# A graph network's first relational layers: residual rows copied DRAM to DRAM, and layer 2's weight sums moved forward

## The chip, the cores and the metric

The kernel runs on one core of a Trainium2 chip. The time is the device time of one execution in microseconds; before the change it is 4654.29 us, the median of three runs (4651.23 to 4654.56). The profile is of one more execution. Its engines are TensorE (PE, with its weight loads as PEld), VectorE (DVE), ScalarE (ACT), GpSimd (POOL), and SyncE (SP), which issues most of the DMAs; POOL issues the indirect ones.

## The reference, cut to what matters

Four blocks are applied in a row to 10000 nodes of 512 features, all in float32: a relational graph network of two layers, a mixture of experts, a second graph network of four layers, and a quantised feed-forward. The change is in the first. With 5000 edges and 2 relations it computes

```python
def rgcn_gate_layer(x, row, col, edge_type, basis, att, gate_w, root, bias):
    w = jnp.einsum('rb,bio->rio', att, basis)      # 2 x 512 x 512 out of 30 bases
    x_j = x[col]
    for r in range(2):
        gate = sigmoid(x_j @ gate_w[r, :, 0])
        msgs.append(gate[:, None] * x_j @ w[r])
    msg = where(edge_type == 0, msgs[0], msgs[1])
    agg = segment_sum(msg, row, num_segments=10000)
    return agg + x @ root + bias

xn = layernorm(x)
h = relu(rgcn_gate_layer(xn, ..., basis1, att1, gate_w1, root1, bias1))
x = x + rgcn_gate_layer(h, ..., basis2, att2, gate_w2, root2, bias2)
```

## The kernel before, in words

**Node rows.** `rgcn_nodes1` goes over 20 blocks of up to 512 nodes. Each block is loaded from the input x (`rows_to`, L139), stored as it is to the DRAM tensor `a2_d` (that store is the "plain rows": the residual x, on which layer 2's results are added later), normalised (L170 to L181), stored to `xn_d`, transposed, multiplied with layer 1's root (L742), given the bias on POOL (L748), and stored to `r1_d`.

**Sorts.** Ahead of the nodes in the text, and interleaved with them in time, the edges are sorted twice by `sort_edges`, by source row and by target row: 40 steps each of small matmuls, ScalarE copies and short VectorE instructions (L334 to L356; L346 is one of these).

**Relation weights.** `relation_weights` (L625 to L638) makes the two 512 x 512 matrices of a layer. For each of 30 bases it loads 1 MB on SP's queue (L630) into one of two buffers and adds it, scaled, to each matrix: one VectorE instruction of 128 x 2048 per matrix (L635 for the first basis, L637 for the others). So there are 60 loads and 120 sums for the two layers.

**Edges.** `rgcn_edges` runs once per layer over 41 tiles of 128 sorted edges. Its loop, whose order on PE, POOL, ACT and DVE is kept as written, has four steps that run on different tiles at a time: `fetch` gathers the source rows by an indirect DMA on POOL (L614; from `xn_d` in layer 1, from `r1_d` in layer 2), six tiles ahead; `make_ready` forms the gates on VectorE and ScalarE (L669 to L682); `add_up` sums rows of the same target by a matmul (L689) and copies the sums on ScalarE (L693); `put` multiplies by the relation's matrix (L703), copies the product (L708) and adds it into DRAM by an indirect DMA on POOL (`scatter_add`, L619; into `r1_d` in layer 1, into `a2_d` in layer 2). After each iteration one step of a side job may be taken, `next(beside)`: steps of `place_nodes`, a generator of short PE and VectorE instructions that lays out rows for the later graph network (L405 to L567).

**Order.** Everything not in such a loop is ordered by a scheduler ahead of the run: each engine has one fixed queue, in which what comes earlier in the program text goes first when it can, and what comes later fills the gaps. Even in the edge loop, instructions from later text can be put between those of the loop. In the text the order is: sorts, nodes, layer 1's weights, layer 1's edges, layer 2's weights, layer 2's edges. SP's queue is one fixed order as well: a load that waits for its buffer holds up what stands behind it.

Of the kernel before, what the change touches and what calls it, by code (L numbers as in the profile page):

```python
# [17 lines left out]
P = 128  # L18
# [24 lines left out]
CAP = 625  # L43
CT = (CAP + P - 1) // P
LAYERS = 4
FETCHED, READY = 6, 3
LN_EPS = 1e-5
BN_EPS = 1e-5
# [21 lines left out]
def gnn_ffn_kernel(ctx: ExitStack, tc: tile.TileContext, I, out, dram):  # L70
# [70 lines left out]
    def row_broadcast(pool, d, width, name):  # L141

        t = pool.tile([P, width], F32, name=name)
        nc.sync.dma_start(t, bass.AP(tensor=d.tensor, offset=d.offset, ap=[[0, P], [1, width]]))
        return t
# [467 lines left out]
    def gather(dst, src, idx):  # L613
        return nc.gpsimd.indirect_dma_start(  # L614
            out=dst, out_offset=None, in_=src, in_offset=bass.IndirectOffsetOnAxis(ap=idx, axis=0)
        )
# [6 lines left out]


    def relation_weights(basis, att_d, pool, stream, tag):  # L625
        att = row_broadcast(pool, att_d, RELATIONS * BASES, f"att_{tag}")
        ws = pool.tile([P, RELATIONS, KC * D], F32, name=f"w_{tag}")
        for b in range(BASES):
            t = stream.tile([P, KC, D], F32, name="basis")
            nc.sync.dma_start(t, basis[b].rearrange("(k p) o -> p k o", p=P))  # L630
            tf = t.rearrange("p k o -> p (k o)")
            for r in range(RELATIONS):
                c = att[:, r * BASES + b : r * BASES + b + 1]
                if b == 0:
                    nc.vector.tensor_scalar(ws[:, r], tf, c, None, op0=OP.mult)  # L635
                else:
                    nc.vector.scalar_tensor_tensor(ws[:, r], tf, c, ws[:, r], op0=OP.mult, op1=OP.add)  # L637
        return ws  # L638

    def rgcn_edges(tag, meta, src_d, relu, ws, gate_d, dst_d, beside, take):  # L640

        with ExitStack() as s:
# [12 lines left out]

            def fetch(t):
                got[t] = wk.tile([P, D], F32, name="x", bufs=FETCHED + 2)
                gather(got[t], src_d, meta["gidx"][:, t : t + 1])  # L660

            def make_ready(t):
                x, kt = got[t], meta["key"][:, t : t + 1]
# [48 lines left out]
            with tc.manual_schedule(engines={E_.PE, E_.Pool, E_.Activation, E_.DVE}):  # L712
                for i in range(RT + FETCHED):
                    if i < RT:
                        fetch(i)
                    if i >= FETCHED - 1 and i - FETCHED + 1 < RT:
                        add_up(i - FETCHED + 1)
                    if i >= FETCHED:
                        put(i - FETCHED)
                    if READY <= i < RT + READY:  # L720
                        make_ready(i - READY)
                    if take(i):
                        next(beside, None)

    def rgcn_nodes1(root, bias, pools):


        ld, tp, small, pt, po = pools
        for b in range(NB):
            tiles, parts, cols = block_tiles(b), block_parts(b), block_cols(b)  # L730
            x = ld.tile([P, 4, D], F32, name="x_in")
            rows_to(x, I["x"], b)
            rows_to(x, a2_d, b, store=True)
            xn = ld.tile([P, 4, D], F32, name="xn")
            layernorm(small, xn, x, tiles, parts, on_act=True)
            rows_to(xn, xn_d, b, store=True)
            xT = transposed(tp, pt, xn, tiles, cols, on_act=True)
            o = tp.tile([P, 4, D], F32, name="o_nodes")
            for a, n in tiles:
                ps_o = po.tile([P, D], F32, name="ps_o")  # L740
                for k in range(KC):
                    nc.tensor.matmul(  # L742
                        ps_o[:n], lhsT=xT[:, k, a * P : a * P + n], rhs=root[:, k, :],
                        start=k == 0, stop=k == KC - 1,
                    )
                nc.scalar.copy(o[:n, a, :], ps_o[:n])
            for n, a0, a1 in parts:
                nc.gpsimd.tensor_tensor(  # L748
                    o[:n, a0:a1], o[:n, a0:a1], bias[:n, None, :].to_broadcast([n, a1 - a0, D]), OP.add
                )  # L750
            rows_to(o, r1_d, b, store=True)

    with ExitStack() as s:
        wpool = s.enter_context(tc.tile_pool(name="w_rel", bufs=1))
        stream = s.enter_context(tc.tile_pool(name="stream", bufs=2))
        src_meta = s.enter_context(tc.tile_pool(name="src_meta", bufs=1))
        wk = s.enter_context(tc.tile_pool(name="sort", bufs=1))
        place_wk = s.enter_context(tc.tile_pool(name="place_wk", bufs=1))
        ps = s.enter_context(tc.tile_pool(name="sort_ps", bufs=2, space=PSUM))
        with ExitStack() as n:  # L760
            ld = n.enter_context(tc.tile_pool(name="ld1", bufs=2))
            tp = n.enter_context(tc.tile_pool(name="tp1", bufs=2))
            fix = n.enter_context(tc.tile_pool(name="fix1", bufs=1))
            small = n.enter_context(tc.tile_pool(name="small1", bufs=3))
            pt = n.enter_context(tc.tile_pool(name="pt1", bufs=2, space=PSUM))
            po = n.enter_context(tc.tile_pool(name="po1", bufs=3, space=PSUM))
            zero = fix.tile([P, D], F32, name="zero")
            nc.gpsimd.memset(zero, 0.0)
            for d in (r1_d, a2_d, xf_d, x2_d):
                clear_spare(zero, d)  # L770
            root = load_square(fix, I["L0_gnn_root1"], "root")
            bias = row_broadcast(fix, I["L0_gnn_bias1"], D, "bias")
            by_src = sort_edges(
                "s", I["src"], I["dst"], I["edge_type_2"], by_src_d, wk, ps, src_meta, by_relation=True
            )
            by_src = add_targets(by_src, wk, ps, src_meta)
            by_dst = sort_edges(
                "d", I["dst"], I["src"], I["edge_weight1"].rearrange("e o -> (e o)"), by_dst_d, wk, ps,
                meta_pool,
            )  # L780
            rgcn_nodes1(root, bias, (ld, tp, small, pt, po))
            ws = relation_weights(I["L0_gnn_basis1"], I["L0_gnn_att1"], wpool, stream, "1")
        placing = place_nodes(by_dst, place_wk, ps, meta_pool)
        rgcn_edges(
            "1", by_src, xn_d, False, ws, I["L0_gnn_gate_w1"], r1_d, placing,
            lambda i: i >= FETCHED and i % 2 == 0,
        )
        ws = relation_weights(I["L0_gnn_basis2"], I["L0_gnn_att2"], wpool, stream, "2")
        rgcn_edges("2", by_src, r1_d, True, ws, I["L0_gnn_gate_w2"], a2_d, placing, lambda i: True)
        for _ in placing:  # L790
            pass

# [1048 lines left out]
```

## Time and profile before

| what | value |
|---|---|
| runs | 4654.29 us median, 4651.23 to 4654.56, three runs |
| profiled execution | 4630.97 us; its span 4629.2 us, mean granted TensorE clock 0.932 |
| busy in the span | PE 4040.4 us (87%), DVE 2791.9 (60%), ACT 1722.2 (37%), POOL 1566.0 (34%) |
| first matmul of the edges, layer 1 | 549.70 us |
| layer 1's edges, first gather to last scatter-add | 532.76 to 840.90 us |
| layer 2's edges, first gather to last scatter-add | 846.62 to 1096.89 us |
| one basis sum (L637) | 2.34 us median, 2.31 to 6.90, 116 of them from 33.2 to 625.0 us |
| SP's queue from 0 to 700 us | 148.03 MB, 62.7% of 16 DMA engines |

The profile shows one execution. A span is the time from its first to its last instruction. "Idle before" an instruction is the time in which its engine did nothing, and the name behind it is what is taken to have ended that; when the engine named had long been done, the wait was for something else, often a DMA. A time "to landing" is from a DMA's issue until its data is there. PE's busy time is modelled, so it can look fuller than it is.

### The profile page before, as it was taken

What the parts mean: (1) busy time and instruction counts of PE and PEld (TensorE: products, weight loads), DVE (VectorE), ACT (ScalarE), POOL (GpSimd) and SP (SyncE); (2) the same over time, 40 slices, a digit from 0 to 9 for tenths busy, and PEclk for the clock granted to TensorE, in tenths of its full rate; (3) what the DMA queues carried; (4) which work ended last, traced back from release to release, by engine and by line L of the source; (5) the groups of instructions that cost most, each with busy time, mean ns of one, the idle gap of its engine ahead of it and who ended that gap; (6) DMA issues with size and microseconds to landing.
All of it is one profiled execution on the core that took longest, in us unless ns stands there. A gap on an engine that the chain in (4) does not pass through costs nothing.

```text
span 4629.2 us, 42910 instructions
## 1 busy us (share of the span) xinstructions
PE 4040.4 (87%) x13624; PEld 2049.1 (44%) x13624; DVE 2791.9 (60%) x5866; ACT 1722.2 (37%) x3082; POOL 1566.0 (34%) x1128
## 2 busy tenths in 40 slices
PE   6799568897999954987788999999999999999997
PEld 4443234443444422443444555545554455544443
DVE  7888864554545456746655557545575455755776
ACT  4334112232333312115545423353233632334775
POOL 3434334342000035875552114211142111422443
PEclk9899789898989876998899999999999999999998
DMA  8677654456555423987521223102231013301332
GB/s 281 227 262 254 215 129 89 82 105 165 197 175 179 153 71 82 163 154 228 176 66 43 78 91 102 37 25 78 97 96 33 30 76 107 88 28 48 109 111 97
DMA packets 294560, 558.83 MB, mean 121 GB/s; under 512 B 41376, under 2 KB 72129, under 8 KB 293311
## 3 DMA queue, kind: packets, MB, share of 16 engines
q1 hardware_dynamic: 221072, 367.30, 23.5%
q0 software_dynamic: 73264, 188.79, 17.7%
q8 instruction: 111, 1.82, 0.2%
q14 instruction: 113, 0.93, 0.1%
HBM read 295.03 MB, written 260.95 MB: 120 GB/s over the span
## 4 chain that ended last, share of the span: by engine, by line
PE 39%; DVE 8%; DMA 3%; ACT 2%; issue 2%; POOL 2%; POOLq 0%; DVEq 0%; ACTq 0%
PE ps_b L1337 15%; PE ps_d L1337 9%; PE ps_o L1613 5%; PE ps_e L1337 4%; PE ps_x L1444 2%; PE ps_x L1268 2%; DMA x<-xg_d,gpos 2%; DVE stats L1422 1%; DMA x_in<-x_d,node_at 1%; PE ps_q L1681 1%; ACT feat L1433 1%; DVE feat L1272 1%; DVE x L1257 1%; DVE feat L1352 1%; DVE t L1360 0%
## 5 line engine op out<-in xcount | busy, mean ns | idle before, releaser
L1337 PE MATMUL ps_b<-feat,w 128*128 128x512 f32 (+1 forms) x1120 | 497.5, 585 | 25.5 <-ACT feat L1433 25.5
L1337 PE MATMUL ps_d<-feat,w_s 128*128 128x512 f32 (+1 forms) x1120 | 503.1, 586 | 2.0 <-ACT p L1345 1.5
L1345 ACT ACTIVATE feat<-ps_b,cols 128x512 f32<-128x512 f32 (+1 forms) x300 | 203.5, 682 | 552.3 <-PE ps_b L1337 539.6
L1372 POOL TENSOR_TENSOR feat<-feat 128x1024 f32<-128x1024 f32 (+1 forms) x70 | 162.6, 2322 | 622.0 <-DVE feat L1371 621.6
L1385 POOL TENSOR_TENSOR feat<-feat,p 128x1024 f32<-128x1024 f32 (+1 forms) x70 | 177.4, 2534 | 482.9 <-ACT feat L1345 482.7
L637 DVE SCALAR_TENSOR_TENSOR w<-basis,att,w 128x2048 f32<-128x2048 f32 x116 | 315.7, 2730 | 15.3 <-DMA basis<-in_L_gnn_basis 15.3
L742 PE MATMUL ps_o<-root,xT 128*128 128x512 f32 (+1 forms) x632 | 322.9, 623 | 0.0
L1337 PEld LDWEIGHTS ps_b<-feat,w 128*128 128x128 f32 x1120 | 208.6, 191 | 256.4 <-issue 209.7
L703 PE MATMUL ps_o<-w,aT 128*128 x656 | 306.8, 612 | 0.1
L1446 DVE TENSOR_TENSOR x_rows<-ps_x,be 128x512 f32<-128x512 f32 (+1 forms) x237 | 157.4, 685 | 230.9 <-PE ps_x L1444 230.9
L1337 PEld LDWEIGHTS ps_d<-feat,w_s 128*128 128x128 f32 x1120 | 203.1, 192 | 199.6 <-issue 176.8
L918 PE MATMUL ps_n<-root,rT 128*128 128x512 f32 (+1 forms) x632 | 287.8, 611 | 0.0
L1337 PE MATMUL ps_b<-t,w_s 128*128 128x512 f32 (+1 forms) x560 | 258.3, 602 | 28.0 <-ACT feat L1345 28.0
L1337 PE MATMUL ps_e<-feat,w 128*128 128x512 f32 (+1 forms) x560 | 259.0, 602 | 9.3 <-DVE feat L1303 9.3
L614 POOL DMA_INDIRECT x<-xg_d,gpos x160 | 179.1, 1120 | 251.4 <-issue 55.2
L1337 PE MATMUL ps_b<-feat,w_s 128*128 128x512 f32 (+1 forms) x560 | 250.2, 586 | 0.0
L1433 ACT ACTIVATE feat<-feat,bn_sm 128x512 f32<-128x512 f32 (+2 forms) x320 | 236.4, 806 | 3.4 <-DVE bn_sm L1552 3.4
L1422 DVE BATCH_NORM_STATS2 stats<-feat 128x6 f32<-128x512 f32 (+1 forms) x320 | 203.0, 667 | 47.6 <-POOL feat L1385 34.6
L1268 PEld LDWEIGHTS ps_x<-same,x 128*128 128x128 f32 x1280 | 165.7, 197 | 106.3 <-ACT x L1263 47.7
L1268 PE MATMUL ps_x<-same,x 128*128 128x128 f32 x1280 | 172.5, 284 | 43.2 <-ACT x L1263 32.0
L1371 DVE TENSOR_TENSOR feat<-feat,t 128x1024 f32<-128x1024 f32 (+1 forms) x70 | 83.8, 1198 | 197.5 <-PE ps_b L1337 197.5
L170 DVE BATCH_NORM_STATS2 ln_st<-x_in 128x6 f32<-128x512 f32 (+1 forms) x237 | 159.5, 682 | 59.3 <-DMA x_in<-x_d,node_at 55.6
(487 smaller groups left out, 7663.9 us busy)
## 6 DMA issues: line engine op xcount, KB each, us to landing
basis<-in_L_gnn_basis SPq DMA_DIRECT2D x60, 1024.0 KB
xg_d<-x_rows SPq DMA_DIRECT2D x234, 256.0 KB
xg_d<-x_in SPq DMA_DIRECT2D x39, 512.0 KB
x_in<-in_x SPq DMA_DIRECT2D x19, 1024.0 KB
a_d<-x_in SPq DMA_DIRECT2D x19, 1024.0 KB
xn_d<-xn SPq DMA_DIRECT2D x19, 1024.0 KB
r_d<-o_nodes SPq DMA_DIRECT2D x19, 1024.0 KB
r_in<-r_d SPq DMA_DIRECT2D x19, 1024.0 KB
```

The lines of the kernel that those rows point to most:

```text
L614: return nc.gpsimd.indirect_dma_start(out=dst, out_offset=None, in_=src, in_offset=bass.IndirectOffsetOnAxis(ap=idx, axis=0))
L637: nc.vector.scalar_tensor_tensor(ws[:, r], tf, c, ws[:, r], op0=OP.mult, op1=OP.add)
L703: nc.tensor.matmul(ps_o, lhsT=aT[:, k, :], rhs=w_all[:, bass.ds(w0 + k * D, D)], start=k == 0, stop=k == KC - 1,)
L742: nc.tensor.matmul(ps_o[:n], lhsT=xT[:, k, a * P : a * P + n], rhs=root[:, k, :], start=k == 0, stop=k == KC - 1,)
L918: nc.tensor.matmul(ps_o[:n_], lhsT=rT[:, k, a * P : a * P + n_], rhs=root[:, k, :], start=k == 0, stop=k == KC - 1,)
L1268: nc.tensor.matmul(ps_a[:, k, :], lhsT=x[:, k * P : (k + 1) * P], rhs=same, start=True, stop=True)
L1337: nc.tensor.matmul(ps[fo], lhsT=A[a][:, k, fo * P : (fo + 1) * P], rhs=x[:, k, :], start=first and k == 0, stop=k == 1, skip_group_check=True,
L1345: nc.scalar.activation(dst[:, fo, :], ps[fo], func, bias=b, scale=scale)
L1385: nc.gpsimd.tensor_tensor(b22, b22, p5, OP.add)
L1422: nc.vector.bn_stats(stats[:, k, 2 * p + j, :], big[:, k, s0 + j * w : s0 + (j + 1) * w])
L1433: nc.scalar.activation(hb, hb, AF.Relu, bias=sm[:, fo, 3:4], scale=sm[:, fo, 2:3])
L1613: nc.tensor.matmul(ps_o[:n_], lhsT=big[:, kc, t * P : t * P + n_], rhs=W2[kc], start=kc == 0, stop=kc == KC - 1,)
```

## The change

There are four edits. (1) The store of plain rows to `a2_d` leaves the node blocks. In its place the first 40 iterations of layer 1's edge loop each issue one DMA on SP's queue from DRAM to DRAM, 250 rows of x into `a2_d`; each waits for the gather that its iteration fetched. (2) `relation_weights` becomes a generator that does one basis per step. Layer 1's 30 and the first 24 of layer 2's are now written ahead of the edge loop, inside the first part. (3) The other six of layer 2's are written into layer 1's edge loop, one in each of the iterations 8, 14, 20, 26, 32 and 38; steps of `place_nodes` are taken in the odd iterations from 7 on, where before it was the even ones from 6 on. Layer 2's edge loop takes a step in every iteration, as before. (4) There are three buffers for bases in place of two.

```diff
+EARLY_BASES = 24
     def relation_weights(basis, att_d, pool, stream, tag):
         att = row_broadcast(pool, att_d, RELATIONS * BASES, f"att_{tag}")
         ws = pool.tile([P, RELATIONS, KC * D], F32, name=f"w_{tag}")
-        for b in range(BASES):
-            t = stream.tile([P, KC, D], F32, name="basis")
-            nc.sync.dma_start(t, basis[b].rearrange("(k p) o -> p k o", p=P))
...
-        return ws
+        def sums():
+            for b in range(BASES):
+                t = stream.tile([P, KC, D], F32, name="basis")
+                nc.sync.dma_start(t, basis[b].rearrange("(k p) o -> p k o", p=P))
...
+                yield
+        return ws, sums()
...
             def fetch(t):
                 got[t] = wk.tile([P, D], F32, name="x", bufs=FETCHED + 2)
-                gather(got[t], src_d, meta["gidx"][:, t : t + 1])
+                return gather(got[t], src_d, meta["gidx"][:, t : t + 1])
...
                 for i in range(RT + FETCHED):
                     if i < RT:
-                        fetch(i)
+                        fetched = fetch(i)
...
-                    if take(i):
-                        next(beside, None)
+                    beside(i, fetched)
...
             rows_to(x, I["x"], b)
-            rows_to(x, a2_d, b, store=True)
...
-        stream = s.enter_context(tc.tile_pool(name="stream", bufs=2))
+        stream = s.enter_context(tc.tile_pool(name="stream", bufs=3))
...
-            ws = relation_weights(I["L0_gnn_basis1"], I["L0_gnn_att1"], wpool, stream, "1")
+            ws1, adding = relation_weights(I["L0_gnn_basis1"], I["L0_gnn_att1"], wpool, stream, "1")
+            for _ in adding:
+                pass
+            ws2, adding = relation_weights(I["L0_gnn_basis2"], I["L0_gnn_att2"], wpool, stream, "2")
+            for _ in range(EARLY_BASES):
+                next(adding)
         placing = place_nodes(by_dst, place_wk, ps, meta_pool)
+        def beside_1(i, ready):
+            if i > FETCHED and i % 6 == 2:
+                next(adding, None)
+            elif i > FETCHED and i % 2:
+                next(placing, None)
+            if i < ET:
+                c0, c1 = N * i // ET, N * (i + 1) // ET
+                cp = nc.sync.dma_start(a2_d[c0:c1, :], I["x"][c0:c1, :])
+                tc.add_manual_dep(
+                    cp.ins, ready.ins.name,
+                    mybir.DependencyInfo(mybir.DependencyClass.Sync, mybir.DependencyReason.DATA),
+                    reason="not all at once, and not beside the nodes",
+                )
+        rgcn_edges("1", by_src, xn_d, False, ws1, I["L0_gnn_gate_w1"], r1_d, beside_1)
+        for _ in adding:
+            pass
         rgcn_edges(
-            "1", by_src, xn_d, False, ws, I["L0_gnn_gate_w1"], r1_d, placing,
-            lambda i: i >= FETCHED and i % 2 == 0,
+            "2", by_src, r1_d, True, ws2, I["L0_gnn_gate_w2"], a2_d, lambda i, _: next(placing, None)
         )
-        ws = relation_weights(I["L0_gnn_basis2"], I["L0_gnn_att2"], wpool, stream, "2")
-        rgcn_edges("2", by_src, r1_d, True, ws, I["L0_gnn_gate_w2"], a2_d, placing, lambda i: True)
```

More of the change, by code (lines that the diff above doesn't have):

```diff
@@ L627, in relation_weights, with rgcn_edges @@
         ws = pool.tile([P, RELATIONS, KC * D], F32, name=f"w_{tag}")
-        for b in range(BASES):
-            t = stream.tile([P, KC, D], F32, name="basis")
[L630 to L637, printed above, removed]
-        return ws
-    def rgcn_edges(tag, meta, src_d, relu, ws, gate_d, dst_d, beside, take):
+        def sums():
+            for b in range(BASES):
+                t = stream.tile([P, KC, D], F32, name="basis")
+                nc.sync.dma_start(t, basis[b].rearrange("(k p) o -> p k o", p=P))
+                tf = t.rearrange("p k o -> p (k o)")
+                for r in range(RELATIONS):
+                    c = att[:, r * BASES + b : r * BASES + b + 1]
+                    if b == 0:
+                        nc.vector.tensor_scalar(ws[:, r], tf, c, None, op0=OP.mult)
+                    else:
+                        nc.vector.scalar_tensor_tensor(ws[:, r], tf, c, ws[:, r], op0=OP.mult, op1=OP.add)
+                yield
+        return ws, sums()
+    def rgcn_edges(tag, meta, src_d, relu, ws, gate_d, dst_d, beside):
         with ExitStack() as s:
```

## The prediction

> **What bounds the kernel now.** I read the windows by stage first, since a share over 4.6 ms says little about a change that ends before 1.1 ms. The columns are busy time (and instructions) of PE, PEld, DVE, ACT and POOL, then granted clock, DMA share and GB/s.
>
> ```profile
> 0.00:408.00 408.00, 339.78 (x1180) 163.87 (x1181) 336.73 (x752) 160.22 (x345) 155.47 (x92) 0.94 0.76 256
> 446.00:532.00 86.00, 63.26 (x189) 29.49 (x187) 66.58 (x41) 22.57 (x41) 33.26 (x9) 0.89 0.69 218
> 532.00:628.00 96.00, 35.35 (x105) 20.01 (x105) 85.83 (x102) 8.49 (x19) 29.19 (x17) 0.64 0.67 201
> 628.00:846.00 218.00, 182.68 (x675) 99.45 (x675) 101.81 (x392) 45.16 (x105) 90.52 (x67) 0.94 0.48 84
> ```
>
> Up to about 510 us TensorE works nearly without a break on the node rows and the two sorts: this is the first part. From 532 to 628 layer 1's edges have begun, but TensorE is busy 35 of 96 us and VectorE 86 of 96; the clock falls to 0.64. After 628 VectorE is half idle. The same windows for the basis sums alone (L637; VectorE busy, instructions) say why:
>
> ```profile
> 408.00:446.00 38.00, 14.02 (x7) 1.00 0.80 273
> 446.00:532.00 86.00, 62.62 (x21) 0.89 0.69 218
> 532.00:628.00 96.00, 73.22 (x32) 0.64 0.67 201
> ```
>
> 32 of layer 2's 60 sums fall into the opening of layer 1's edges, between the edge instructions of the same engine. SyncE's queue shows it too: 15 of the 60 basis loads are issued from 528 to 616 us.
>
> ```profile
> 522.15 1.14 SPq L139 DMA_DIRECT2D r_d<-o_nodes  x2
> 528.18 87.95 SPq L630 DMA_DIRECT2D basis<-in_L_gnn_basis  x15
> ```
>
> Then the timeline of POOL, for what sets the pace of the edges once VectorE is free (start, duration, instruction, idle time before it):
>
> ```profile
> 532.76 3.00 POOL L614 DMA_INDIRECT x<-xn_d,gidx_s  x1 [17.95 <-DVE w L637]
> ...
> 818.84 1.58 POOL L619 DMA_INDIRECT r_d<-o,sidx  x1 [4.00 <-DMA r_d<-o,sidx]
> 824.34 1.55 POOL L619 DMA_INDIRECT r_d<-o,sidx  x1 [3.92 <-issue]
> 829.89 1.55 POOL L619 DMA_INDIRECT r_d<-o,sidx  x1 [4.00 <-ACT o L708]
> 835.35 1.55 POOL L619 DMA_INDIRECT r_d<-o,sidx  x1 [3.92 <-issue]
> 840.90 1.55 POOL L619 DMA_INDIRECT r_d<-o,sidx  x1 [4.00 <-DMA r_d<-o,sidx]
> 846.62 1.01 POOL L614 DMA_INDIRECT x<-r_d,gidx_s  x1 [4.18 <-DMA r_d<-o,sidx]
> ```
>
> The last six scatter-adds have no gathers between them and still start 5.5 us apart: 1.55 of issue and 4.0 of waiting. The engines named differ from row to row and the wait doesn't, so it is the landing of the scatter before, which adds into the same DRAM tensor. The free stage runs at this pace with gathers too, one tile per 5.5 to 5.7 us. So layer 1's edges are bound twice: by VectorE to 628 us, then by a chain of scatter-adds.
>
> **The change part by part.** All sums are made against the profiled execution (4630.97 us; span 4629.2 and 1.8 around it). The median of the runs is 4654.29, 23.3 above it, and I carry a difference over unchanged. A change under 0.2% (9.3 us) can't be told from none here.
>
> *Bases out of the opening of the edges.* Before, 34 sums (17 bases) were left when the edges opened: 86 us (541 to 627) in which 8 tiles were made ready (eight pairs of L669), 5.06 us a base. At the free pace 8 tiles cost 8 x 5.55 = 44 us, so the bases cost 42 us. The two layers agree: from first to last scatter-add layer 1 takes 840.90 - 566.37 = 274.5 us and layer 2, with as many tiles, 1096.89 - 867.00 = 229.9, 44.6 less. If n early bases are still unsummed when the edges open, n x 5.06 us pass in which 0.47 n tiles are made ready, so the saving is 42 - 2.45 n. Six bases go to single tiles. So n is 17 - 6 = 11 if the first part takes no more than before (15 us saved), and 0 if all of the 24 fit (42 saved; 58 from first gather to last scatter-add by layer 2's length, 250.3 against 308.1, since the ramp to the first scatter-add also shrinks from 33.6 to 20.4 us). Does the first part have room? Up to 510 us VectorE is busy about 410, so about 100 are idle, and 11 bases need 22 x 2.34 = 51. Half of the idle time lies in gaps of 1 to 2 us behind TensorE's sort products, shorter than a sum; the start and the waits for the sorted lists can't be filled. I take n = 5: **-29 us**, ends -15 and -58.
>
> *Third basis buffer.* L637 waits 15.3 us for loads in all, 11 times; with one more load in flight the waits before the edges (6.8 us) shrink. It also frees SyncE: the last two r_d stores stood behind a basis load at 521.73 that waited for its buffer, though POOL had finished the rows at 514.8. Gathers could start some us earlier: **-3 us**, ends 0 and -8.
>
> *More sums in the first part.* TensorE there waits 22.1 us for L346, a short sort instruction that on VectorE can stand behind a 2.34 us sum. Twelve more sums among the sorts at up to 1.2 us each would be 15; most of the added ones come after the sorts end at 446. I take **+3**, ends 0 and +15.
>
> *Plain rows out of the first part.* 21 stores of up to 1 MB (20.5 MB) leave SyncE's queue and the engines. In that part TensorE waits for no input row (0.7 us of VectorE waits for x_in in all), so I book nothing; the relief is part of the room for n.
>
> *Forty copies beside layer 1's edges.* Each moves 250 rows, 512 KB, from x to a2_d, and waits in SyncE's queue for gather i to land. Behind the waiting copy stand the loads of the last six bases and layer 2's gate; a wait lasts at most one tile, and three of the six loads find free buffers early, so I cost it at nothing; were each of the six sums to wait one tile, 33 us. Layer 2's scatter-adds need all copies, but the last gather is issued at 804 and the first of these scatter-adds at 867, so 60 us cover it. What is dear is the scatter chain, which stands at 5.5 us with the DMA engines half busy. Gathers land 4.3 us after issue, and one is issued 1.9 us after each scatter-add, so a copy is issued 6.2 us after one scatter-add, that is 0.7 us after the next: it runs while that one is in flight. No row shows a DRAM-to-DRAM copy. Two rows bound it:
>
> ```profile
> 820.38 0.34 SPq L144 DMA_DIRECT2D gate<-in_L_gnn_gate_w  x1
> ```
> ```profile
> 1030.46 0.37 SPq L149 DMA_DIRECT2D root<-in_L_gnn_root  x1
> ```
> ```profile
> 1031.63 1.58 POOL L619 DMA_INDIRECT a_d<-o,sidx  x1 [2.90 <-ACT o L708]
> 1033.52 0.99 POOL L614 DMA_INDIRECT x<-r_d,gidx_s  x1 [0.30 <-issue]
> 1041.21 1.59 POOL L619 DMA_INDIRECT a_d<-o,sidx  x1 [6.70 <-ACT o L708]
> ```
>
> The gate load, 512 KB like a copy, was issued 1.5 us after the scatter-add of 818.84, and the next came 5.5 us after it: no delay. Root, bias and the small loads behind them (some 1.6 MB) began 1.2 us before a scatter-add, which landed after 8.8 us instead of 4.8: 4.0 more, 2.5 us per MB, so 1.3 us for half a MB. Here a rule speaks against the change. The Trainium skill ("DMA: Bandwidth & Descriptors", section "Why a DMA increments its semaphore by 16 and not by 1") says that a transfer uses as many engines, up to 16, as divide its slowest dimension. 250 rows would give 10. The first 700 us moved 148.03 MB on SyncE's queue for 62.7% of 16 engines, 21 GB/s an engine; ten engines then need 2.4 us a copy, not 1.5, and as a scatter-add is complete only with its slowest engine, it could wait up to 2.4 us. The same page ("Queues, rings and completion order") has an engine drain a packet of some 9 to 17 descriptors of one queue before it turns to the other: 16 rows of 2 KB are 1.5 us. By these rules 34 copies (seven are released by the first gathers, before any scatter-add) cost 34 x 1.5 = 51 us or more, up to 82; by the gate row nothing. The trace can't decide, as no load there has 250 rows. I take a value near the gate row, for it has the copy's size and nearly its phase, and because the chain gives way: a copy that delays a gather comes later behind the next scatter-add. 0.2 us each: **+7 us**, ends 0 and +82.
>
> *Late bases.* Six times two sums, 4.7 us, on VectorE in tiles without a placing step. VectorE waits 2.4 to 3.3 us per tile there for ScalarE's gate; the rest, up to 2.3, reaches an activation with one tile of slack. **+4**, ends 0 and +14.
>
> Sum: -29 - 3 + 3 + 7 + 4 = **-18 us**: 4613 for a profiled execution, 4636 for the median.
>
> **The rivals.** (1) *The copies lengthen the scatter chain.* For it: the 8.8 us landing, the two rules, the engines half busy already. Against: the gate row, and the opening of the edges itself, where basis loads ran at 200 GB/s and two scatter-adds landed after 5.0 and 5.4. At 1.5 us a copy: -18 - 7 + 51 = +26, 4680; it decides from 25 / 34 = 0.74 us a copy, and at 2.4 gives +57. (2) *The early bases don't fit.* n stays 11 and the sums slow the sorts: -15 - 3 + 15 + 7 + 4 = +8 at worst, -4 with the sorts unharmed; about 4655. For it: VectorE is at 83% there already and its order is fixed before the run. The change then doesn't do what it says, for the edges open as crowded as before. (3) *All 24 fit and the ramp shrinks*: -58 + 3 + 7 + 4 - 3 = -47, 4607. For it: 100 us of idle VectorE and 20 MB less to move. (4) *A late basis load stands behind copies* and VectorE stops the edges: up to +33 on my sum, +15, 4669.
>
> **How the numbers follow.** My sum 0.42, rival 1 0.24, rival 2 0.17, rival 3 0.12, rival 4 0.05. Faster by over 0.2%: 0.38 of mine, 0.12 of (3), 0.04 of (2): 0.54. Within 0.2%: 0.04 of mine, 0.08 of (2), 0.02 of (1): 0.14. Slower: 0.32. The predicted time is my sum's, 4636; its own range is 4620 to 4646. The range reaches to rival 3 below, 4600, and above to rival 1 at about 1.8 us a copy, 4690.
>
> **What would show it.** The windows from the first gather: TensorE busy well over 35 of its first 96 us, and a clock above 0.64. L637: few sums between the first gather and the first ten scatter-adds, then pairs six tiles apart. First to last scatter-add of layer 1: 245 to 255 us instead of 274.5. The scatter-adds 5.5 to 5.9 us apart beside the copies; 7 or more shows rival 1. The first gather between 522 and 540; later, with more TensorE waits for L346, shows rival 2. VectorE waiting for a basis load inside the edges shows rival 4. I am wrong if layer 1's edges end later than 846 us.

## The result, and the profile after

The changed kernel takes 4638.22 us (median of 20 runs, 4629.52 to 4653.54) against 4651.83 us of the kernel before on the same chip (20 runs, 4641.55 to 4670.19). The ratio is 0.9974 with a 95% interval of 0.9965 to 0.9983, or 8 to 16 us less. The forecast was 4636 us. It is right as a total, and that by luck: three of its terms are wrong, and they cancel.

Single executions scatter by some 10 us, and the two profiled ones don't show the gain (4637.62 us after, 4630.97 before; the last section has what is known of the reason). So I compare stages by their marks, in us from the start of the span. The line numbers of the changed kernel: basis load L634, basis sum L641, gather L615, scatter-add L620, copy L801.

| mark | before | after | difference |
|---|---|---|---|
| last bias addition of the node rows ends | 514.8 | 517.1 | +2.3 |
| first gather of layer 1 | 532.76 | 531.84 | -0.9 |
| first scatter-add of layer 1 | 566.37 | 549.08 | -17.3 |
| last scatter-add of layer 1 | 840.90 | 824.58 | -16.3 |
| median spacing of these scatter-adds | 5.70 | 6.66 | +0.96 |
| last scatter-add of layer 2 | 1096.89 | 1074.96 | -21.9 |

The marks are of one execution each, and by the end of layer 2 they show more than the 8 to 16 us that the timed runs gain.

First the windows by stage of the changed kernel, with the columns as before (busy time and instructions of PE, PEld, DVE, ACT and POOL; granted clock, DMA share, GB/s):

```profile
0.00:408.00 408.00, 339.90 (x1187) 166.64 (x1188) 369.49 (x755) 160.24 (x340) 145.98 (x88) 0.96 0.72 244
446.00:532.00 86.00, 66.23 (x191) 27.63 (x190) 65.66 (x68) 20.22 (x42) 37.29 (x16) 0.90 0.68 220
532.00:628.00 96.00, 75.28 (x269) 43.74 (x270) 48.90 (x169) 19.85 (x45) 40.74 (x31) 0.88 0.69 182
628.00:846.00 218.00, 149.75 (x536) 83.78 (x535) 106.50 (x336) 38.08 (x87) 86.78 (x59) 0.84 0.59 141
```

The opening of the edges has changed as foreseen: TensorE is busy 75 of 96 us where it was 35, at a clock of 0.88 where it was 0.64. The room was found in the first 408 us: VectorE is busy 369 us there (337 before), and TensorE no less than before. The stage after 628 has become slower: TensorE does 536 matmuls in 218 us where it did 675, since fewer of layer 1's 41 scatter-adds are left for it (28, where it had 36) and they come further apart. The DMA engines are busy 0.59 of it, up from 0.48.

The basis sums alone, in the same kernel (VectorE busy, instructions):

```profile
0.00:408.00 408.00, 197.07 (x76) 0.96 0.72 244
408.00:446.00 38.00, 21.65 (x8) 0.96 0.58 202
446.00:532.00 86.00, 59.87 (x22) 0.90 0.68 220
532.00:628.00 96.00, 9.21 (x4) 0.88 0.69 182
```

In the kernel before, 58 sums lay in the first 408 us (165.84 us of VectorE); now 76 do. The 24 early bases are all summed when the first gather goes; the four sums from 532 to 628 are the first two of the six late bases. So all 24 fit, as rival 3 had it.

SyncE's queue and the scatter-adds on POOL, where one late basis is loaded:

```profile
535.34 141.22 SPq L801 DMA_DIRECT2D a_d<-in_x  x26
676.66 0.53 SPq L634 DMA_DIRECT2D basis<-in_L_gnn_basis  x1
685.27 35.22 SPq L801 DMA_DIRECT2D a_d<-in_x  x6
720.58 0.54 SPq L634 DMA_DIRECT2D basis<-in_L_gnn_basis  x1
```
```profile
662.85 1.59 POOL L620 DMA_INDIRECT r_d<-o,sidx  x1 [3.79 <-DMA r_d<-o,sidx]
...
669.41 1.59 POOL L620 DMA_INDIRECT r_d<-o,sidx  x1 [3.68 <-DVE eq L213]
...
675.97 1.59 POOL L620 DMA_INDIRECT r_d<-o,sidx  x1 [3.52 <-ACT aT L699]
...
685.42 3.24 POOL L620 DMA_INDIRECT r_d<-o,sidx  x1 [6.57 <-DMA r_d<-o,sidx]
```

Scatter-adds beside copies start 6.56 us apart here, and the one after the basis load of 676.66 starts 9.45 us after its predecessor. That next one takes 3.24 us to issue in place of 1.59, while VectorE does the two sums (684.84 to 689.46 us); so it is with each scatter-add whose issue starts during a sum in this kernel (2.86 to 3.24 us). In the waits of the stage, the scatter-add's for its predecessor and VectorE's for a late basis both have a row (total, times, longest):

```profile
POOL r_d L620 <- DMA r_d<-o,sidx: 60.3, 15, 6.6
...
DVE w L641 <- DMA basis<-in_L_gnn_basis: 19.6, 3, 9.3
```

So rival 1 (copies lengthen the chain) is there at 0.96 us a copy, and rival 4 (VectorE waits for a late load) three times, 9.3, 5.4 and 4.9 us.

To put a price on each, I take what every gap between layer 1's scatter-adds has over the undisturbed 5.7 us and add these up. Before: 46.5 us, of which 43.1 in the first twelve gaps (sums in the opening, single gaps of 22 and 24 us). After: 47.5 us, spread over the stage. Sums out of the opening therefore gave 17.3 + 43.1 = 60 us, and what was new beside the edges cost 47.5 - 3.4 = 44. The difference is the 16 us by which layer 1 ends earlier.

Not all of these 44 us belong to copies and late bases. Two gaps near the end are 9.21 us (beside the last copy and small loads, `sw` and `sb`, that the kernel before issued in layer 2's edges) and 8.43 us (beside no transfer; a `place_nodes` instruction of 3.45 us on VectorE covers the start of POOL's issue, which takes 4.46 us). The two hold 6.2 us over the pace.

### The profile page after: what moved, and what is told of

It reads as the page before. It is cut to its first block, busy times and chain, and to the rows that moved or that the text cites. A ratio compares the mean times of both kernels' runs of the same rounds, so it can differ in the third digit from the quotient of the medians.

```text
span 4635.8 us, 42956 instructions
## 1 busy us (share of the span) xinstructions
PE 4036.5 (87%) x13624; PEld 2049.5 (44%) x13624; DVE 2788.0 (60%) x5866; ACT 1724.1 (37%) x3082; POOL 1560.6 (34%) x1128
## 3 DMA queue, kind: packets, MB, share of 16 engines
q1 hardware_dynamic: 212016, 367.30, 23.5%
## 4 chain that ended last, share of the span: by engine, by line
PE 38%; DVE 8%; DMA 3%; issue 2%; ACT 2%; POOL 2%; POOLq 0%; DVEq 0%; ACTq 0%
PE ps_b L1361 15%; PE ps_d L1361 9%; PE ps_o L1637 5%; PE ps_e L1361 4%; PE ps_x L1468 2%; PE ps_x L1292 2%; DMA x<-xg_d,gpos 2%; DVE stats L1446 1%; DMA x_in<-x_d,node_at 1%; PE ps_q L1705 1%; DVE feat L1296 1%; ACT feat L1457 1%; DVE feat L1376 1%; DVE x L1281 1%; DVE t L1384 1%
## 5 line engine op out<-in xcount | busy, mean ns | idle before, releaser
L1361 PE MATMUL ps_b<-feat,w 128*128 128x512 f32 (+1 forms) x1120 | 497.5, 585 | 25.6 <-ACT feat L1457 25.6
L641 DVE SCALAR_TENSOR_TENSOR w<-basis,att,w 128x2048 f32<-128x2048 f32 x116 | 306.2, 2651 | 19.6 <-DMA basis<-in_L_gnn_basis 19.6
L615 POOL DMA_INDIRECT x<-xg_d,gpos x160 | 178.6, 1116 | 256.7 <-PE ps_x L1292 50.4
```

Source lines behind the costliest of these rows:

```text
L615: return nc.gpsimd.indirect_dma_start(out=dst, out_offset=None, in_=src, in_offset=bass.IndirectOffsetOnAxis(ap=idx, axis=0))
L1361: nc.tensor.matmul(ps[fo], lhsT=A[a][:, k, fo * P : (fo + 1) * P], rhs=x[:, k, :], start=first and k == 0, stop=k == 1, skip_group_check=True,
```

## Experiments

Every time is a median, with the ratio to the kernel before on the same chip; edits are to the changed kernel unless said otherwise.

**The stores back, no copies**

```diff
             rows_to(x, I["x"], b)
+            rows_to(x, a2_d, b, store=True)
...
-                cp = nc.sync.dma_start(a2_d[c0:c1, :], I["x"][c0:c1, :])
```

> The changed kernel without its forty copies: the plain rows are stored from the node blocks again, the bases stay as changed (24 early, six late, three buffers). My theory, from the two traces: the bases gave some 58 us and the copies took some 35 of it back, by stretching the distance of layer 1's scatter-adds from 5.5 to 6.5 us; if so, the distance returns to 5.5 to 5.7 us, the first to the last scatter-add takes 235 to 245 us in place of 275, and the kernel takes about 4605 us, if the 24 bases still fit beside the stores. If the stores took the room that the bases need, four to eight sums stand in the opening of the edges and the time is 4615 to 4635. Rival, copies are free and the late bases stretch the chain: the distance stays at 6.5 us and the time at 4638.

Measured: 4658.7 us, ratio 1.0005 (0.9994 to 1.0017). The spacing falls to 5.705, as expected; the rest is a miss. The first scatter-add comes at 587.01, 38 us later than in the changed kernel, as the sums pile up ahead of it:

```profile
0.00:408.00 408.00, 163.49 (x58) 0.94 0.76 258
...
532.00:560.00 28.00, 28.00 (x13) 0.50 0.93 302
560.00:590.00 30.00, 11.51 (x6) 0.61 0.79 257
```

These sums hold POOL too. They run almost without a break from 541.93 to 566.89 us, and the first gather takes 21.72 us to issue; in the changed kernel it took 1.02:

```profile
546.06 21.72 POOL L615 DMA_INDIRECT x<-xn_d,gidx_s  x1 [22.04 <-DMA r_d<-o_nodes]
```
```profile
531.84 1.02 POOL L615 DMA_INDIRECT x<-xn_d,gidx_s  x1 [14.76 <-DMA r_d<-o_nodes]
```

The first part holds 58 sums again and not 76. The removal of the stores, which I had booked at nothing, is what let the sums in. Without copies the excess over 5.7 us is 27.0. Of this 17.9 lie in four gaps of 9.2 to 11.2 us, each right behind the two sums of a late basis, and 5.3 in two gaps of 8.3 and 8.5 us without a sum beside them.

**Copies alone, on the kernel before**

```diff
-            rows_to(x, a2_d, b, store=True)
...
+                cp = nc.sync.dma_start(a2_d[c0:c1, :], I["x"][c0:c1, :])
```

> The kernel before with the copies alone: plain rows go DRAM to DRAM beside layer 1's edges, the bases as before with two buffers. If the copies cost 1 us per tile, the scatter-adds after the opening stand 6.5 us apart, layer 1's first to last scatter-add takes 295 to 310 us in place of 274.5, and the kernel is 15 to 35 us slower than before. Rival, copies are free: 275 us and no difference; if the stores had held up the node blocks, 5 to 10 us faster.

Measured: 4690.73 us, ratio 1.0074 (1.0048 to 1.0100), 34 us more and at the upper edge of what was expected, but not where it was expected. Spacing 6.615: the copies cost the same where no basis load is issued beside them (none from 564 to 801 us). Layer 1's first to last scatter-add, expected at 295 to 310 us, takes 271.14, since fewer sums are left in its opening; the last scatter-add comes 10.1 us later than before. Layer 2's first comes 28.2 us later (895.23): six basis loads are issued only from 801.6 us on, behind the copies in SyncE's queue. With two buffers and all sums of layer 2 written behind layer 1's edges, the room that the stores left was used for six more sums only (64 in 408 us).

**Copies in small pieces**

```diff
-                c0, c1 = N * i // ET, N * (i + 1) // ET
-                cp = nc.sync.dma_start(a2_d[c0:c1, :], I["x"][c0:c1, :])
+                c0, c1 = 256 * i, min(256 * (i + 1), N)
+                cp = nc.sync.dma_start(
+                    a2_d[c0:c1, :].rearrange("(r p) d -> p r d", p=16),
+                    I["x"][c0:c1, :].rearrange("(r p) d -> p r d", p=16),
+                )
```

> The changed kernel with the copies cut otherwise: 256 rows each (the last one 16), as 16 times 16 separate rows of 2 KB, where the copies before are 16 contiguous pieces of 32000 bytes. The bytes are the same. If a scatter-add waits behind large pieces on each DMA engine, small ones let it through sooner: 5.6 to 6.0 us apart, first to last 250 to 260 us, the kernel 15 to 25 us below 4638. Rival, it is the bytes that share the engines: 6.5 us and 4638 as before, or slower by some us for the many small pieces.

Measured: 4646.56 us, ratio 0.9976 (0.9967 to 0.9984); spacing 6.74. Rows of 2 KB cost as much as pieces of 32,000 bytes: the size of a piece is not what the scatter-add waits for.

**All 30 bases early**

```diff
-EARLY_BASES = 24
+EARLY_BASES = 30
```

> The changed kernel with all 30 of layer 2's bases in the first part and none in the edge tiles. If the three waits of VectorE for late loads (9.3, 4.9 and 5.4 us) cost what the scatter gaps of 8.6 to 9.9 us show, some 10 us come back. If the first part is full, the other six bases (six times 4.7 us on VectorE) put off the opening of the edges by up to 28 us, or stand in it. I expect the sum at +5 to +15 us; rival, there is still room in the first part: 8 to 12 us faster than 4638.

Measured: 4646.54 us, ratio 0.9982 (0.9970 to 0.9993). The intervals of this kernel and the changed one overlap, so the split of 24 and six is worth little either way. The trace shows what is exchanged: 13 sums fill 28.00 of the 28 us from 532 to 560 and the first scatter-add comes at 579.67, while the excess over 5.7 us falls to 35.8. Less the 3.4 that was there before, 32 us are left beside the copies (30 without one `place_nodes` gap of 8.53 us), and taking the late bases out saves 47.5 - 35.8 = 12 us. The other order of taking out gives another split: taking the copies out (the stores back) saves 47.5 - 27.0 = 20 us, and 27.0 - 3.4 = 24 are left (18 without the two gaps that have no sum beside them). So of the 44 us the copies' share is 20 to 30 and the late bases' 12 to 18; the two overlap.

**Loads ahead.** Each basis is loaded two bases ahead of its sums.

```diff
+            load(0)
+            load(1)
             for b in range(BASES):
-                t = stream.tile([P, KC, D], F32, name="basis")
-                nc.sync.dma_start(t, basis[b].rearrange("(k p) o -> p k o", p=P))
+                if b + 2 < BASES:
+                    load(b + 2)
+                t = loaded.pop(0)
```

> The changed kernel with each basis loaded two sums ahead (its load is written before the sums of the basis two before it, three buffers as now). The late loads then stand in SP's queue ahead of the copies of twelve tiles, and the data lies ready. If VectorE's three waits for a late basis (9.3, 4.9 and 5.4 us) are what made the three long gaps between scatters (9.45, 9.92 and 8.61 us against 6.66), no wait on a basis load is left inside layer 1's edges, no gap there is over 7.5 us because of a basis, and the time falls by 6 to 12 us (to about 4629). If the long gaps come from the sums themselves (4.6 us of VectorE in one tile), gaps of 8 us and more stay and the time is within 3 us of the changed kernel.

Measured: 4622.78 us (four runs), ratio 0.9955 (0.9939 to 0.9972). Waits go as the first theory has it, the gaps as the second; the time is as the first, though its interval overlaps the changed kernel's. VectorE waits for no basis in the stage, yet there are still three gaps of 9.27, 9.85 and 10.53 us, at the three loads. The wait and the long gap were two effects of one load, and removing the wait did not remove the gap. The profiled execution is the longest of the four (4639.34) and its opening runs 12 us late, so it doesn't show where the gain comes from.

**Copies at another phase.** Copy i waits for the scatter-add of tile i - 6 to land, not for its own gather.

```diff
-                        put(i - FETCHED)
+                        fetched = put(i - FETCHED)
```

> The changed kernel with each copy from tile 6 on released by the landing of the scatter-add six tiles back instead of by the landing of its gather, so that it starts while GpSimd issues the next scatter-add (1.6 us) and not in the middle of a flight. If what a copy costs depends on when it starts, the median spacing of layer 1's scatters falls from 6.66 to 5.7-6.1 us and the time by 15 to 30 us. If the copy's bytes take their time on the 16 engines whenever they go, spacing stays at 6.5-6.8 us and the time within 6 us of the changed kernel.

Measured: 4630.5 us, ratio 0.9975 (0.9966 to 0.9983). The spacing falls from 6.66 to 5.93, so most of a copy's price is its timing: the same 512 KB cost 0.2 us in the middle gap. The DMA packets in the traces show why. The table has medians over layer 1's gaps, in us:

| kernel | POOL begins the issue to first packet of the scatter-add | first to last packet | last packet to next issue | first packet of the copy, from the same issue |
|---|---|---|---|---|
| before | 2.16 | 2.34 | 1.12 | none |
| changed | 2.84 | 2.57 | 1.12 | 1.2 |
| this one | 2.19 | 2.43 | 1.11 | 0.5 |

Some 0.6 us decide: the earlier copy is mostly through when the scatter-add's packets start, and the later one puts them off by 0.7 us. The time stays all the same. The late loads still stand behind copies, VectorE waits for them three times (20.5 us, up to 7.9), and the gaps behind those sums have grown to 12.54, 13.93 and 13.84 us.

**Half of the copies in the first part; all of them there** (the edit of the second, which has no copy beside the edges; the first copies half as many rows there, and 125 a tile beside the edges)

```diff
             rows_to(x, I["x"], b)
+            c0, c1 = N * b // NB, N * (b + 1) // NB
+            nc.sync.dma_start(a2_d[c0:c1, :], I["x"][c0:c1, :])
```

> The changed kernel with half of the plain rows copied DRAM to DRAM in the first part (one copy of 250 rows beside each of the 20 node blocks, which waits for nothing) and the other half beside the edges, 125 rows (256 KB) a tile instead of 250 (512 KB). If a copy's price is by its bytes, the median spacing is (5.70+6.66)/2 = 6.2 us, 6.0 to 6.4. If it is by the copy (its issue, its descriptors' start), it stays at 6.5 or more. If only the first kilobytes collide, 5.8 or less.

> The changed kernel with all plain rows copied DRAM to DRAM in the first part, one copy of 500 rows (1 MB) written beside each node block's load and waiting for nothing, and no copy beside the edges. It moves as many bytes in the first part as the loads and stores of the kernel with stores put back (20 MB written; that one took the first scatter from 549 to 587 us, and layer 2's end to 1094). If stores hurt the first part because they stand in SP's queue and wait for their block's data, so that basis loads come late behind them, this kernel keeps the early sums (first scatter at 549 to 556) and has a spacing of 5.7: time 4638 - 37 = about 4601, 4595 to 4615. If the bytes themselves crowd the first part, the first scatter comes at 570 to 590 and the time is 4640 to 4665, like the kernel with the stores.

Measured: 4867.66 us (1.0486, 1.0469 to 1.0504) and 5129.83 us (1.1048, 1.1029 to 1.1067). Both times missed widely, and for a reason that no theory had: in both kernels no basis is loaded until the nodes are done. With all the copies in the first part (sums alone):

```profile
0.00:760.00 760.00, 0.00 (x0) 0.78 0.31 107
760.00:1040.00 280.00, 219.97 (x98) 0.54 0.67 224
```

The DMA engines are busy 0.31 of these 760 us, so it isn't bytes. The order of SyncE's queue is fixed ahead of the run, and with a DRAM-to-DRAM copy in each node block the scheduler put the basis loads behind the nodes (the first one at 802.0 us). The nodes themselves last to 801.16 us in place of 517.1: SyncE's queue waits 492.8 us for rows that it is to store, and VectorE 408.5 us for input rows that stand behind them. The spacings can still be read: 5.63 with no copies beside the edges, 6.02 with copies of 256 KB, 6.66 with 512 KB. The middle one lies in the range by bytes, near its lower end; with 256 KB the scatter-add's first packet comes at 2.37 us, between the 2.16 and 2.84 above.

**Two basis buffers**

```diff
-        stream = s.enter_context(tc.tile_pool(name="stream", bufs=3))
+        stream = s.enter_context(tc.tile_pool(name="stream", bufs=2))
```

> The changed kernel with two basis buffers instead of three. The third buffer was booked at -3 us (0 to -8). If it is worth no more than that, the sums in the first 408 us stay at 74 to 76 instructions, the first scatter at 549 to 552 us, and the time 0 to 8 us above the changed kernel. If it carries a large part of the sums that moved into the first part, sums in the first 408 us fall towards 65, the first scatter comes at 560 to 580, and the time rises by 10 to 25 us.

Measured: 4674.43 us, ratio 1.0057 (1.0041 to 1.0073): slower than the kernel before. Against the changed kernel's 0.9974 the third buffer is worth 0.83%, about 39 us. The trace has it in two places: the first scatter-add at 575.56 instead of 549.08 (26.5), and 287.3 us from the first to the last instead of 275.5 (11.8). Sums in the first 408 us:

```profile
0.00:408.00 408.00, 171.09 (x65) 0.94 0.65 221
```

Set beside the others this makes a small table of sums in 408 us: stores and two buffers (before) 58, stores and three 58, no stores and two 65, no stores and three 76. Neither edit does much alone. (The first of the four also has layer 2's sums later in the program; the changed kernel with stores and two buffers was not run.)

**Both edits: loads ahead and copies at the other phase**

```diff
+                if b + 2 < BASES:
+                    load(b + 2)
...
-                        put(i - FETCHED)
+                        fetched = put(i - FETCHED)
```

> Both edits on the changed kernel: each basis loaded two sums ahead, and each copy from tile 6 on released by the landing of the scatter-add six tiles back. With the copies on that release alone the median spacing fell to 5.93 us, but the late loads behind them made gaps of 12.5 to 13.9 us; with the loads ahead alone the waits for a basis were gone. If the two add up, spacing 5.9, gaps of 8 to 10 us only where a late basis is summed, first to last scatter 255 to 265 us instead of 275.5, and 4612 to 4624 us against the changed kernel's 4638. If the loads ahead only move the wait (the load stands behind another copy), gaps of 12 us and more stay and the time is no lower than the better of the two alone (ratio to before 0.9955).

Measured: 4622.88 us (six runs), ratio 0.9938 (0.9925 to 0.9951), the fastest of all and below the changed kernel's interval. First to last scatter-add 257.05 us, spacing 6.1, longest gap 9.4. It is as expected, save that the spacing is a little above 5.9: a copy costs 0.4 us here. Behind the sums of a late basis with no load beside it the gaps are 7.69, 8.03 and 6.80 us, with a load 8.69 to 9.40.

**Both, with the late bases summed one relation at a time**

```diff
+                    if r == 0:
+                        yield
...
-            if i > FETCHED and i % 6 == 2:
+            if i > FETCHED and i % 3 == 2:
```

> As the kernel with both edits (loads two sums ahead, copies on the scatter's landing), and the late bases are summed one relation at a time: 2.3 us of VectorE in every third tile instead of 4.6 us in every sixth. If the long gaps with loads ahead (9.3 to 10.5 us) come from the 4.6 us of sums standing ahead of the next tile's gate products on VectorE, then no gap is over 8.5 us, and the time falls by another 4 to 12 us. If the price is by the total of sums and not by their length in one tile, the long gaps become twice as many at half the excess and the time is within 4 us of the kernel with both edits.

Measured: 4624.92 us, ratio 0.9953 (0.9939 to 0.9966), no gain. It says what the longest gaps are. SyncE's queue (line numbers of this kernel) and POOL around one of them:

```profile
599.99 0.49 SPq L813 DMA_DIRECT2D a_d<-in_x  x1
600.57 0.54 SPq L636 DMA_DIRECT2D basis<-in_L_gnn_basis  x1
608.99 0.49 SPq L813 DMA_DIRECT2D a_d<-in_x  x1
```
```profile
600.74 1.59 POOL L620 DMA_INDIRECT r_d<-o,sidx  x1 [2.48 <-DVE eq L213]
...
609.74 1.59 POOL L620 DMA_INDIRECT r_d<-o,sidx  x1 [6.09 <-DMA r_d<-o,sidx]
...
615.89 1.59 POOL L620 DMA_INDIRECT r_d<-o,sidx  x1 [1.62 <-ACT o L726]
```

No sum runs in that gap; the next one starts at 611.06. The scatter-add issued at 600.74 is done at about 609.7. A copy and the 1 MB of the basis were issued just ahead of it; its own packets start 5.38 us after its issue, where 2.16 is usual, and 0.06 us before the load's last packet ends. In the other two, and in the changed kernel's three, they start at most 0.3 us before it. There are three such gaps (9.0, 10.01, 9.54), one for each load inside the edges; the first three late bases lie in the buffers already. Where sums run, in the other tiles, no gap is over 7.4.

**Copies in the first part, on POOL's queue** (none beside the edges)

```diff
             rows_to(o, r1_d, b, store=True)
+            c0, c1 = N * b // NB, N * (b + 1) // NB
+            nc.gpsimd.dma_start(a2_d[c0:c1, :], I["x"][c0:c1, :])
```

> The changed kernel with all plain rows copied DRAM to DRAM in the first part, one copy of 500 rows (1 MB) behind each node block, issued by GpSimd on its own queue and not by SyncE, and no copy beside the edges. With the copies on SyncE's queue in the first part, the planner had put nearly all basis loads behind the nodes, and nothing could be read on the bytes; in this one the basis loads stand as early in SyncE's order as in the changed kernel (57 of 60 ahead of the last node block's store). If the 20 MB fit beside the first part's traffic, sums in the first 408 us stay at 70 to 76 instructions, the first scatter comes at 545 to 560, spacing is 5.7, and the time 4600 to 4620. If the bytes themselves crowd the first part (as the stores seemed to), the sums in 408 us fall to about 60, the first scatter comes at 570 to 590, and the time is 4630 to 4660.

Measured: 4702.09 us, ratio 1.0109 (1.0092 to 1.0125), slower than both theories allow.

```profile
0.00:408.00 408.00, 212.25 (x80) 0.91 0.78 268
```

The sums fit even with the copies' bytes (80 in 408 us), and the edges run as the first theory has it (spacing 5.70). But the node rows end at 608.97 instead of 517.1, with the sorts waiting longer: POOL waits 138 and 140 us for the sorted positions in the two sorts, where it was 75 and 83. So 20 MB more beside the sums don't keep them out, though TensorE is behind with the nodes there (busy 312 of the 408 us, 340 in the changed kernel). What the bytes add to the 92 us, and what the other order does, isn't told apart.

## Why the prediction was right, and where it wasn't

**Bases out of the opening**: -29 forecast, about -60 measured, which is the far end that I had given for n = 0 (-58). The failed step is "I take n = 5": n was 0. I had counted half of VectorE's idle time as gaps too short for a sum; VectorE now fills 369 of the first 408 us and TensorE still loses almost nothing. One reading below it was off as well: 30 sums (15 bases) start from 541 us on, not 34, which makes 5.7 us a base and not 5.06; at n = 0 that changes nothing. And VectorE was not the whole of what bound the opening: its sums also held POOL's issues, as the row of 21.72 us shows.

**Third buffer** (-3) **and stores out** (0): the same mistake from the other side. I priced each by the waits visible before (6.8 us for basis loads, 0.7 for input rows), not by what the scheduler does with the room. With the stores there three buffers leave the early sums at 58, and without them the third buffer is worth about 39 us. The stores' removal brings the first scatter-add 38 us forward (587.01 to 549.08); with them back the time is about 14 us higher although the copies are gone. These sums are part of the 60, not beside it. Why the stores keep sums out (their place in SyncE's queue, the scheduler's price for them, or their bytes) isn't settled.

**More sums in the first part**: +3 forecast. TensorE waits 25.6 us for the short sort instruction (22.1 before), the node rows end 2.3 us later. Right.

**Forty copies**: +7 forecast, 20 to 30 measured. The failed step is "it has the copy's size and nearly its phase". The gate row's phase was another one: its packets start 3.87 us after the issue of the scatter-add at 818.84, behind that one's own, which start at 2.15 us; the copies' start at 1.2 us, ahead of them. Nor did the chain give way as I argued. A copy costs 0.96 us at the middle gap, past the 0.74 from which rival 1 was to decide; it didn't, because the bases gave twice what I had booked. (The scatter-adds with a copy beside them number 33, as seven of 40 go ahead, not 34.) Of the two rules I weighed, the one on dividing 250 rows over ten engines (the Trainium skill, "DMA: Bandwidth & Descriptors", section "Why a DMA increments its semaphore by 16 and not by 1") did not come into play, for the trace has each copy as 16 packets of 32,000 bytes. The other (same page, section "Queues, rings and completion order"), on a packet of some 9 to 17 descriptors of one queue being drained before the next, is not tested: cut into rows of 2 KB a copy has 16 of them an engine, which may be one packet, so that the rule makes the two cuts alike, as measured. My estimate from it, 1.5 us a copy, was too high. Phase is what the runs show: on the other release the price is 0.2 to 0.4 us.

**Late bases**: +4 forecast for the sums and nothing for the loads; 12 to 18 measured. The failed step is "I cost it at nothing". The three tiles with a load (9.45, 9.92 and 8.61 us against 6.66) hold 8 us. It was not the wait in SyncE's queue (rival 4) that made them: 1 MB going ahead of a scatter-add's packets holds that one for 2 to 4 us, wait or no wait. The sums of a basis with no load beside them cost 0.3 to 0.7 us in the gap behind them at a pace of 6.6, where there is more slack, 0.7 to 1.9 at 6.1, and up to 4.7 at 5.7 (the stores back); which fits that copies and late bases together cost less than the sum of the two alone.

**Layer 2** was not booked. It gains 5.6 us over layer 1's end, 4.6 of them from its first to its last scatter-add (225.3 us, 229.9 before): the root and bias loads, which had landed beside a scatter-add that took 8.8 us, now go at 487 and 510 us. The two kernels that still issue them in layer 2's edges (copies alone, two basis buffers) still take 229.3 and 229.4 us there.

In sum for layer 1: -60 for the bases and +44 for copies and late bases together (with the 6 us of other gaps in it) are -16. My own terms gave -18 for the whole. From the first to the last scatter-add I had said 245 to 255 us; it is 275.5, one of the marks that showed at once that the sum was right for wrong reasons. The gain stayed small because rival 3 (the sums fit) and rival 1 (the copies lengthen the chain) both came true.

## What to carry to other kernels

A resource edit (a buffer, a store taken away) in front of a stage scheduled ahead of the run can't be priced by the waits visible before: ask how much work waits to move into the room, and price edits that act on the same room together. A chain of scatter-adds into one tensor pays for transfers whose packets go ahead of its own; start such transfers early enough to be nearly over when the next link's packets start, and take large loads out of the stage. Check a sum by its stage marks, since a right total can hide three wrong terms.

## What was not expected of the hardware

The same 512 KB copy between two DRAM tensors costs a chain of 256 KB scatter-adds 0.96 us when it is released by a gather and 0.2 to 0.4 us when it is released by the landing of a scatter-add, some 0.6 us earlier against the next one's packets.

An indirect DMA that POOL issues while VectorE runs basis sums back to back is not through its issue until they are over: 21.72 and 19.00 us for one gather in two kernels with many sums in the opening (stores back, all 30 early), against 1.02. I had not counted with it; that the sums are the cause is read from the times, and no run here was made to test it.

Between 1740 and 1785 us, far behind the change, the profiled execution of the changed kernel has two long idle times of TensorE, 10.7 us (with no releaser named) and 14.5 us. First the waits around them after the change (1714 to 1800 us), then in the same stretch before (1736 to 1822 us):

```profile
PE ps_c L1107 <- DVE ind L1121: 19.1, 10, 2.0
PE ps_c L1107 <- issue: 17.5, 6, 10.7
PE ps_c L1107 <- DVE sel L1121: 14.5, 1, 14.5
```
```profile
PE ps_c L1083 <- DVE ind L1097: 27.0, 16, 2.1
...
PE ps_c L1083 <- DVE sel L1097: 2.0, 1, 2.0
```

From the first hidden-layer matmul of the experts block (about 1123 us after, 1145 before) to the first of the second graph network's wide matmuls the kernel before took 964.2 us in its profiled execution, and the changed kernel and all twelve of the experiments 985.5 to 993.8, the one made from the kernel before (copies alone) among them with 991.8 (its two idle times in that place are 11.7 and 14.6 us). These 23.5 us are why the profiled spans don't show the gain: added to the execution before, they would set it 17 us above the one after, an estimate near the upper end of the timed 8 to 16. The profiled execution of before lies below all 20 timed ones shown with it (4630.97 against 4641.55 and more), which points to a lucky execution and not to the change. The cause of the idle times stays open.
